# A macaron block's attention maxima: rows by transfers inside SBUF, small steps spread, sums split, two tiles normalized early

## The chip, the cores and the metric

The kernel runs on one core of a Trainium2 chip. The metric is device time in microseconds (us) from the first to the last instruction of an execution, median of the runs. Five engines work side by side, each with its own queue of instructions in a fixed order: TensorE (PE; its weight loads are PEld), VectorE (DVE), ScalarE (ACT), GpSimd (POOL) and SyncE (SP, which here only issues transfers). DMA transfers issued on SP run in the hardware queue q1, those issued on POOL in the software queue q0.

## The reference

Input x is 4 x 1024 x 512 (batches, tokens, width), float32. A half feed-forward, attention and a second half feed-forward follow one another, each on normalized rows and added to x:

```
x = x + 0.5 * ffn(layernorm(x))
x = x + attention(layernorm(x))        # 32 query heads of 16, 8 key heads, rope, softmax
x = x + 0.5 * ffn(layernorm(x))
# ffn: h = silu(x @ Wg') * (x @ Wu');  hn = h * rsqrt(mean(h*h) + eps);  hn @ Wp'
#      Wg', Wu', Wp': bf16 weights, ternary by groups of 64; hidden width 2048
# attention: w = softmax(q k^T / 4) over 1024 keys; each key head serves a group of 4 query heads
```

## The kernel before, in words

Work goes by batch b = 0 to 3. A round has three stages: a feed-forward stage (`FeedForward`) of up to three blocks of 512 tokens, the heads of attention (`Attention.run`), and a stage that projects the old attention's output and makes the next batch's queries, keys and values (`input_output`; `output` after the last). A special first feed-forward (`First`) quantizes the weights. Inside each stage the order of all engines' instructions is written out by hand (`manual_schedule`), so an engine waits where its next instruction waits.

**The heads.** The stage has 128 steps: 8 groups g of four query heads, two halves of 512 queries (qh), 8 tiles of 128 keys (kc). In step n, TensorE makes scores `s` for two pairs of heads (L1273; 512 queries by 128 keys, transposed), ScalarE takes the exponential of each pair (`e`, L1282), and TensorE weighs the values with the exponentials of the step before (eight `o` matmuls, L1289). In the first step of each half of a group, TensorE also adds the row maxima into the scores' banks: a matmul of `pick` with `even_rows` (even groups) or `odd_rows` (odd groups). Those tiles hold, in the partitions 0 to 3 and 64 to 67, minus the maximum of each query and head as a row of 1024 queries, as a high and a low part.

**The maxima.** The maxima of later groups are found ahead. `maxima` (L1126) is one item: a TensorE matmul of 128 queries by 512 keys into a bank `sm` (three of them in the heads) and a VectorE reduction to one column of `pm` (L1147). `pattern` (L1310) puts three items into each step; `more` and `READY` add a fourth if the items lag. The maxima of groups 0, 1 and most of 2 are found beside the feed-forward (`early`). When a group's 64 items are done, `subtract_maxima` (groups 0 to 5) reduces `pm` (L1169), writes high and low parts to `mst` (L1172, L1173) and leaves a function `turn` to the next step: TensorE transposes to 64 rows (`pmT`, L1181), VectorE copies them (`mrow`, L1183), POOL writes them to DRAM (`d_m`, L1185), and a later step's `maxima_in` reads them into the rows by four POOL transfers (L1221). `turn_half` (groups 6 and 7, by halves of the queries) instead puts the parts into columns of a cleared tile `spread`, transposes four 128x128 tiles (L1208) and copies the result whole into the rows (L1209), with no transfer. The two halves of group 6 are turned in steps 95 and 96, and step 96 reads the first.

**Around the heads.** SP's queue holds, in program order, the loads of the ring's places (`p_m`, `p_s`, `p_in`, `p_out`), the stores `d_o` of finished outputs, and the small transfers of `divide` (`den`, `d_r`, `rec`). Eight steps before the end, `normal_rows` makes the first token tile of the next batch (L1323); the other tiles are normalized in `input_output`, tile 1 in its first pass (L847), just ahead of its transposes (L130).

**A feed-forward's tail.** `chunks` ends with the projections of the last two hidden chunks into four banks `po` (L339 to L345). After the second bank, `factors` (L253) sums the squares of h: eight matmuls of `acc` and `sq` with a column of ones into `pq` (L259), then three small steps to the factor `half`, which `end` needs (L282).

Of the kernel before, what the change touches and what calls it, by code (L numbers as in the profile page):

```python
# [19 lines left out]
P = 128  # L20
# [17 lines left out]
def tile_macaron_block(  # L38
# [96 lines left out]
    class FeedForward:  # L135
# [116 lines left out]

        def factors(self, k):  # L253

            label = f"{self.label}_{k}"
            pq = self.ps.tile([P, 4], F32, tag="gu", name=f"pq_{label}")
            for i in range(4):
                for n, acc in enumerate(self.accs[k]):
                    nc.tensor.matmul(  # L259
                        pq[:, i : i + 1],  # L260
                        lhsT=acc[:, i * P : (i + 1) * P],
                        rhs=ones,
                        start=(n == 0),
                        stop=(n == len(self.accs[k]) - 1),
                    )
            ms = small.tile([P, 4], F32, tag="ms", name=f"ms_{label}")
            nc.vector.tensor_scalar(ms, pq, 1.0 / H, RMS_EPS, ALU.mult, ALU.add)
            inv = small.tile([P, 4], F32, tag="inv", name=f"inv_{label}")
            inverse_root(inv, ms, 4)
            half = small.tile([P, 4], F32, tag="half", name=f"half_{label}")  # L270
            nc.vector.tensor_scalar(half, inv, 0.5, None, ALU.mult)
            return half
# [33 lines left out]
        def chunks(self):  # L306
# [31 lines left out]

            for i in range(4):  # L339
                for behind in due:  # L340
                    self.project(*behind, [i])
                if i == 1:
                    half = self.factors(k)
# [4 lines left out]
    class First(FeedForward):  # L348
# [29 lines left out]
        def projection(self):  # L378

            with tc.manual_schedule():  # L380
                for c in range(2):
                    self.split(c)
                    self.parts[1, c][1]()
                for c in range(HC):
                    if c + 2 < HC:
                        self.split(c + 2)
                    self.project(1, c, self.parts[1, c][0], [0, 1])
                    self.project(1, c, self.parts[1, c][0], [2, 3])
                    if c + 2 < HC:
                        self.parts[1, c + 2][1]()  # L390
                    if 6 <= c < 10:
                        load_x(2, c - 6)
                    if c == 2:
                        at[0].first_rows()
                    if c == HC - 2:
                        half = self.factors(1)
                self.end(1, half)
# [429 lines left out]
    def input_output(new, old, put, then, wp, ps):  # L827
        turn, banks = None, 2 if put is None else 1
        puts = {4: (0,), 5: (1,), 6: (2,), 7: (3,), 8: (4,), 9: (5, 6, 7)}
        for n in range(NT + 2):  # L830
# [16 lines left out]
            if scales is not None:  # L847
                new.normalize(n + 1, wp, scales)
# [48 lines left out]
    class Attention:  # L897
# [19 lines left out]
        READY = (HKV - 1) * STEPS + NT - 3  # L917
# [3 lines left out]
        def __init__(self, b):  # L921
# [12 lines left out]
            self.early_rows = None  # L934
            self.rows, self.xTs, self.made = {}, {}, {}
            self.turning = []
# [10 lines left out]
        def first_rows(self):  # L947
# [6 lines left out]
            self.early_rows = rows  # L954

        def scales(self, i):

            if i == 0 and self.early_rows is not None:
                return None
            return normal_scales([xt[self.b, i]], f"a_{self.b}_{i}")  # L960

        def normalize(self, i, wp, scales):
            if scales is None:
                self.rows[i] = self.early_rows
# [161 lines left out]
        def maxima(self, j, ps, bufs):  # L1126
# [19 lines left out]
            def end():  # L1146
# [3 lines left out]
                done, rest = divmod(min(self.ended), self.ITEMS)  # L1150
                if min(self.ended) == before:
                    return
                if rest == self.ITEMS // 2 and g == HKV - 1:
                    self.turn_half(g, 0)
                elif rest == 0:
                    if g < HKV - 2:
                        self.subtract_maxima(g, ps, bufs)
                    else:
                        for part in range(g == HKV - 1, 2):
                            self.turn_half(g, part)  # L1160
# [4 lines left out]
        def subtract_maxima(self, g, ps, bufs):  # L1165

            b = self.b
            m = small.tile([P, NT, G], F32, tag="m", name=f"m_{b}_{g}", bufs=2)
            nc.vector.tensor_reduce(m, self.pm[g], AX.X, ALU.max, negate=True)  # L1169
            mst = small.tile([P, G, 2, NT], F32, tag="mst", name=f"mst_{b}_{g}", bufs=2)  # L1170
            by_head = m.rearrange("p i j -> p j i")
            nc.vector.tensor_copy(mst[:, :, 0, :].bitcast(F32R), by_head)  # L1172
            nc.vector.tensor_tensor(  # L1173
                mst[:, :, 1, :].bitcast(F32R), by_head, mst[:, :, 0, :], ALU.subtract
            )
            rows = G * 2 * NT
            tag = "sm" if bufs < 4 else "gu"

            def turn():
                pt = ps.tile([P, 512], F32, tag=tag, name=f"pmT_{b}_{g}", bufs=bufs)  # L1180
                nc.tensor.transpose(pt[:rows, :P], mst.rearrange("p j r i -> p (j r i)"), ident)  # L1181
                mrow = small.tile([rows, P], F32R, tag="mrow", name=f"mrow_{b}_{g}", bufs=2)
                nc.vector.tensor_copy(mrow, pt[:rows, :P])  # L1183
                self.mT[g] = dram.tile([rows, P], F32, tag="d_m", name=f"d_m_{b}_{g}", bufs=HKV)
                nc.gpsimd.dma_start(self.mT[g], mrow.bitcast(F32))  # L1185
                if g == 0:
                    self.maxima_in(g)

            self.turning.append(turn)

        def turn_half(self, g, part):

            tiles = slice(part * 4, part * 4 + 4)
            m = small.tile([P, 4, G], F32, tag="m", name=f"m_{self.b}_{g}_{part}", bufs=2)
            nc.vector.tensor_reduce(m, self.pm[g][:, tiles], AX.X, ALU.max, negate=True)
            columns = self.spread[:, tiles].rearrange("p i (e s) -> p i e s", s=PAIR)[..., :4]
            high, low = (columns[..., r::2] for r in range(2))
            m = m.rearrange("p i (a e) -> p i e a", e=2)  # L1200
            nc.vector.tensor_copy(high.bitcast(F32R), m)
            nc.vector.tensor_tensor(low.bitcast(F32R), m, high, ALU.subtract)

            def turn():
                t = self.mrows[g] = self.odd_rows if g % 2 else even_rows
                pt = self.ps.tile([P, 512], F32, tag="sm", name=f"pmT_{self.b}_{g}_{part}", bufs=3)
                for i in range(4):
                    nc.tensor.transpose(pt[:, i * P : (i + 1) * P], self.spread[:, part * 4 + i, :], ident)  # L1208
                nc.vector.tensor_copy(t[:, part * 512 : (part + 1) * 512], pt)  # L1209

            self.turning += [None, turn] if g == HKV - 1 else [turn]
# [38 lines left out]
        def run(self, keep, wp, ps):  # L1250
# [3 lines left out]
            self.spread = wp.tile([P, NT, P], F32, tag="spread", name=f"spread_{b}", bufs=1)  # L1254
# [56 lines left out]
            more = (0, 5, 10, 15)  # L1311
            late = None
            places.load(("t2", b + 1) if b + 1 < B else ("out", B))
            for n in range(HKV * self.STEPS):
# [7 lines left out]
                if n == HKV * self.STEPS - 8 and b + 1 < B:  # L1322
                    (at[b + 1].early_rows,) = normal_rows(  # L1323
                        [xt[b + 1, 0]], f"a_{b + 1}_0", keep, "rec"
                    )
                turn = self.turning.pop(0) if self.turning else None
                sides = list(pattern[n % 4]) if n > 0 else [(), ()]
                if n > 0 and n % 16 in more and self.TOTAL - sum(self.counts) > 3 * (self.READY - n):
                    sides[1] += (sides[1][0] ^ 1,)
# [7 lines left out]
                for end in ends:  # L1337
                    end()
                if late is not None:
# [5 lines left out]
                if n == 1:  # L1345
                    nc.gpsimd.memset(self.spread, 0.0)
# [111 lines left out]
```

## Time and profile before

| | us |
|---|---|
| time, median of 3 runs (lowest, highest) | 3199.89 (3199.06, 3209.4) |
| the profiled execution | 3200.95 |
| its span, from the first to the last instruction in the trace | 3199.2 |
| heads stages, from the first `o` matmuls to the last, rounds 0 to 3 | 281.7, 281.4, 281.8, 280.8 |
| TensorE busy in the window 635.5:921 (heads of round 0) | 281.58 of 285.50 |
| VectorE, ScalarE busy there | 229.95, 253.55 |
| reduction `pm<-sm` (L1147), one | 0.68 |
| `pmT<-ident,spread` (L1208), one of 64 | 0.27 |
| copy into `even_rows` or `odd_rows` (L1209), one of 16 | 0.69 |
| copy `mrow` (L1183), one of 24 | 0.28 |
| `d_m<-mrow`, issue to landing, median | 4.7 |
| rows from `d_m`, issue to landing, median (slowest) | 4.5 to 4.7 (6.3) |

The granted TensorE clock is 0.99 over the span and 1.00 in the heads. In timeline lines the columns are start, duration, engine, source line, operation, output<-inputs, shapes and count; square brackets give the engine's idle time before and what ended it.

### The profile page before, as it was taken

To read this page: it belongs to the slowest core of one execution; us is meant where nothing else is said; L and a number is where in the kernel's file an instruction comes from. 1 tells how busy PE (TensorE), PEld (TensorE's weight loads), DVE (VectorE), ACT (ScalarE), POOL (GpSimd) and SP (SyncE) were. 2 spreads that over 40 slices of the span, in tenths; PEclk is the share of its full clock that TensorE was granted. 3 is DMA by queue.
4 is the path that set the end of the run, shared out by engine and by line. 5 is a ranking of instruction groups with operands and counts; after the bars stand their busy time and mean duration, and the time that the engine had idled before them with its cause. 6 is when DMAs were issued, how large, how long until landed. Compare 5 with 4: busy or idle time off the path is not lost. (4 is left out here: it accounts for less than half of the span.)

```text
span 3199.2 us, 46128 instructions
## 1 busy us (share of the span) xinstructions
PE 3112.0 (97%) x16944; PEld 1963.6 (61%) x16944; DVE 2188.1 (68%) x3659; ACT 1758.5 (55%) x2346; POOL 951.0 (30%) x932
## 2 busy tenths in 40 slices
PE   5999899999999999999999999999999999999999
PEld 4777677733358777533377777433487776333687
DVE  7976566588855666688756665888556666887243
ACT  5752333389852333689823333898623335888343
POOL 2564333300034343201053333110243332010344
PEclk8999999999999999999999999999999999999999
DMA  3543222224324133133333222133241231332111
GB/s 111 161 125 97 88 61 78 62 76 120 111 82 129 53 93 109 45 117 102 91 107 96 87 73 70 70 110 115 86 130 60 76 96 61 97 120 65 41 60 42
DMA packets 229522, 285.64 MB, mean 89 GB/s; under 512 B 29296, under 2 KB 174704, under 8 KB 229296
## 3 DMA queue, kind: packets, MB, share of 16 engines
q1 hardware_dynamic: 220784, 271.66, 27.4%
q0 software_dynamic: 8512, 11.03, 1.6%
q8 instruction: 134, 2.20, 0.3%
q14 instruction: 92, 0.75, 0.1%
HBM read 215.74 MB, written 66.85 MB: 88 GB/s over the span
## 5 line engine op out<-in xcount | busy, mean ns | idle before, releaser
L1147 DVE TENSOR_REDUCE pm<-sm 128x1 f32<-128x512 f32 x2048 | 1281.1, 683 | 213.5 <-PE sm L1138 211.3
L1282 ACT ACTIVATE e<-s 128x1024 f32<-128x1024 f32 x1024 | 991.6, 1024 | 147.4 <-PE s L1273 138.9
L205 PE MATMUL gu<-xT,guT 128*128 128x512 f32 x1792 | 710.0, 396 | 9.9 <-DVE ql L1064 8.3
L205 PE MATMUL gu<-xL,guT 128*128 128x512 f32 x1792 | 703.2, 392 | 0.4 <-DVE xL L133 0.4
L1289 PE MATMUL o<-e,vs 128*32 128x512 f32 x4096 | 548.1, 604 | 0.0
L1138 PE MATMUL sm<-p_m,p_m 64*128 64x512 f32 x2048 | 497.1, 412 | 8.8 <-DVE h L217 6.0
L1273 PEld LDWEIGHTS s<-p_s,p_s 64*128 64x128 f32 x2048 | 193.0, 183 | 485.5 <-ACT e L1282 467.7
L1273 PE MATMUL s<-p_s,p_s 64*128 64x512 f32 x2048 | 469.0, 451 | 9.6 <-ACT e L1282 9.6
L225 POOL TENSOR_TENSOR sq<-h 128x512 f32<-128x512 f32 x210 | 218.5, 1041 | 724.1 <-DVE h L217 724.1
L217 DVE TENSOR_TENSOR h<-sg,gu 128x512 f32<-128x512 f32 x224 | 153.7, 686 | 381.2 <-PE gu L205 370.5
L215 ACT ACTIVATE sg<-gu 128x512 f32<-128x512 f32 x224 | 134.2, 599 | 480.6 <-PE gu L205 480.5
L205 PEld LDWEIGHTS gu<-xT,guT 128*128 128x128 f32 x1792 | 339.6, 190 | 84.9 <-ACT guT L94 8.7
L205 PEld LDWEIGHTS gu<-xL,guT 128*128 128x128 f32 x1792 | 339.4, 189 | 72.5 <-DVE xL L133 1.2
L245 PE MATMUL po<-w_pT,high 128*128 128x512 f32 x896 | 374.8, 418 | 0.7 <-DVE x L282 0.7
L245 PE MATMUL po<-w_pT,low 128*128 128x512 f32 x896 | 356.7, 398 | 0.2
L231 ACT CAST high<-h 128x512 fp32r<-128x512 f32 x224 | 139.1, 621 | 335.4 <-DVE h L217 323.5
L1138 PEld LDWEIGHTS sm<-p_m,p_m 64*128 64x128 f32 x2048 | 227.9, 185 | 93.9 <-DVE h L217 49.9
L229 POOL TENSOR_TENSOR acc<-acc,sq 128x512 f32<-128x512 f32 x205 | 275.8, 1346 | 16.0
L94 ACT CAST guT<-g 128x512 fp32r<-128x512 bf16 x448 | 275.0, 614 | 8.0 <-ACT guT L94 5.5
L245 PEld LDWEIGHTS po<-w_pT,high 128*128 128x128 f32 x896 | 168.7, 188 | 94.4 <-issue 56.4
L233 DVE TENSOR_TENSOR low<-h,high 128x512 fp32r<-128x512 f32 x224 | 168.6, 753 | 40.9 <-ACT high L231 40.9
L1289 PEld LDWEIGHTS o<-e,vs 128*32 128x32 f32 x4096 | 81.2, 108 | 180.9 <-issue 155.2
(166 smaller groups left out, 2934.9 us busy)
## 6 DMA issues: line engine op xcount, KB each, us to landing
g<-d_guT SPq DMA_DIRECT2D x448, 128.0 KB
p_m<-d_q SPq DMA_DIRECT2D x56, 512.0 KB
p_s<-d_q SPq DMA_DIRECT2D x56, 512.0 KB
d_o<-oT SPq DMA_DIRECT2D x64, 256.0 KB
p_m<-d_km SPq DMA_DIRECT2D x28, 512.0 KB
p_s<-d_ks SPq DMA_DIRECT2D x28, 512.0 KB
x<-in_L_attn_x_dram SPq DMA_DIRECT2D x32, 256.0 KB
w<-in_L_ffn_w_gate_up_dram SPq DMA_DIRECT2D x32, 256.0 KB
```

What stands on the lines that cost most here:

```text
L94: nc.scalar.copy(w, t)
L205: nc.tensor.matmul(pg, lhsT=self.weights[k, hc][part][:, c, :], rhs=xp[:, c, :], start=(c == 0 and low == 0), stop=(c == DC - 1 and low == 1),
L217: nc.vector.tensor_tensor(h, sg, gu[1], ALU.mult)
L225: nc.gpsimd.tensor_tensor(sq, h, h, ALU.mult)
L229: nc.gpsimd.tensor_tensor(acc, acc, sq, ALU.add)
L233: return (high, low), lambda: nc.vector.tensor_tensor(low, h, high.bitcast(F32), ALU.subtract)
L245: nc.tensor.matmul(self.pos[k][i], lhsT=h[:, i * P : (i + 1) * P], rhs=w_pT[hc], start=(hc == 0 and n == 0), stop=(hc == HC - 1 and n == 1),)
L1138: nc.tensor.matmul(s, lhsT=q[j // 2][at, i * P : (i + 1) * P], rhs=k[at, half * 512 : (half + 1) * 512], start=True, stop=True,)
L1147: nc.vector.tensor_reduce(pm[:, i, j, half : half + 1], s, AX.X, ALU.max)
L1273: nc.tensor.matmul(s[:, e, :], lhsT=lhsT[at], rhs=rhs[at, queries], start=(kc == 0 and n == 0), stop=(n == len(terms) - 1), skip_group_che ...
L1282: return w, lambda: nc.scalar.activation(w, s, AF.Exp, scale=1.0 / HD**0.5)
L1289: nc.tensor.matmul(o[j * SLOT : (j + 1) * SLOT, :], lhsT=vs[:, kc, g, :], rhs=es[j // 2][:, j % 2, :], start=(kc == 0), stop=(kc == NT - 1),)
```

## The change

Five edits:

- *Rows inside SBUF.* `turn_half` and `spread` go. Groups 3 to 7 turn through `subtract_maxima`: one transpose, one copy `mrow`, and four transfers on SP from `mrow` straight into the rows. Groups 6 and 7 do so by halves (32 rows). Groups 0 to 2 still go through DRAM.
- *Chores.* For groups 3 to 6 the three small VectorE steps are put off, one per step of the heads (`chores`), the transpose one step after the third. Groups 0 to 2 and 7 do them at once.
- *The fourth item* (`more`, `READY`) goes.
- *Two tiles early.* Where the heads normalized one tile of the next batch they now normalize two (`rows_ahead`).
- *Sums split.* In the tail of the last block of a stage, the four matmuls on `acc` come before the last projections, the four on `sq` where all eight were (`sums`). In `First.projection` both are issued in the same place as before.

```diff
+        def sums(self, k, n):
+            if n == 0:
+                self.pq = self.ps.tile([P, 4], F32, tag="gu", name=f"pq_{self.label}_{k}")
+            for i in range(4):
+                nc.tensor.matmul(
+                    self.pq[:, i : i + 1],
+                    lhsT=self.accs[k][n][:, i * P : (i + 1) * P],
+                    rhs=ones,
+                    start=(n == 0 and i == 0),
+                    stop=(n == len(self.accs[k]) - 1),
+                    skip_group_check=True,
+                )
         def factors(self, k):
...
-            pq = self.ps.tile([P, 4], F32, tag="gu", name=f"pq_{label}")
-            for i in range(4):
-                for n, acc in enumerate(self.accs[k]):
-                    nc.tensor.matmul(
-                        pq[:, i : i + 1],
-                        lhsT=acc[:, i * P : (i + 1) * P],
-                        rhs=ones,
-                        start=(n == 0),
-                        stop=(n == len(self.accs[k]) - 1),
-                    )
+            self.sums(k, len(self.accs[k]) - 1)
+            pq = self.pq
...
+            if len(self.accs[k]) > 1:
+                self.sums(k, 0)
...
+                        self.sums(1, 0)
...
-            if scales is not None:
+            if n + 1 < NT:
...
-        READY = (HKV - 1) * STEPS + NT - 3
...
-            self.early_rows = None
+            self.early_rows = {}
...
-            self.turning = []
+            self.turning, self.chores = [], []
...
-            self.early_rows = rows
+            self.early_rows = {0: rows}
+        def rows_ahead(self, keep):
+            tiles = [xt[self.b, i] for i in range(2)]
+            mv, rstd = normal_scales(tiles, f"a_{self.b}_0")
+            rows = keep.tile([P, 2, D], F32, tag="rec", name=f"xn_a_{self.b}_0", bufs=1)
+            for i, t in enumerate(tiles):
+                nc.vector.tensor_scalar(
+                    rows[:, i], t, mv[:, i, 0:1], rstd[:, i : i + 1], ALU.subtract, ALU.mult
+                )
+                self.early_rows[i] = rows[:, i]
...
-            if i == 0 and self.early_rows is not None:
+            if i in self.early_rows:
...
-                self.rows[i] = self.early_rows
+                self.rows[i] = self.early_rows[i]
...
-                done, rest = divmod(min(self.ended), self.ITEMS)
-                if min(self.ended) == before:
+                g, rest = divmod(min(self.ended) - 1, self.ITEMS)
+                if min(self.ended) == before or rest % (self.ITEMS // 2) != self.ITEMS // 2 - 1:
...
-                if rest == self.ITEMS // 2 and g == HKV - 1:
-                    self.turn_half(g, 0)
-                elif rest == 0:
-                    if g < HKV - 2:
-                        self.subtract_maxima(g, ps, bufs)
-                    else:
-                        for part in range(g == HKV - 1, 2):
-                            self.turn_half(g, part)
+                part = rest // (self.ITEMS // 2)
+                if g >= HKV - 2:
+                    self.subtract_maxima(g, ps, bufs, part)
+                elif part == 1:
+                    self.subtract_maxima(g, ps, bufs)
+                if part == 1:
...
-        def subtract_maxima(self, g, ps, bufs):
+        def subtract_maxima(self, g, ps, bufs, half=None):
...
-            m = small.tile([P, NT, G], F32, tag="m", name=f"m_{b}_{g}", bufs=2)
-            nc.vector.tensor_reduce(m, self.pm[g], AX.X, ALU.max, negate=True)
-            mst = small.tile([P, G, 2, NT], F32, tag="mst", name=f"mst_{b}_{g}", bufs=2)
+            n = NT if half is None else NT // 2
+            first = 0 if half is None else half * n
+            label = f"{b}_{g}_{first}"
+            m = small.tile([P, n, G], F32, tag="m", name=f"m_{label}", bufs=2)
+            mst = small.tile([P, G, 2, n], F32, tag="mst", name=f"mst_{label}", bufs=2)
...
-            nc.vector.tensor_copy(mst[:, :, 0, :].bitcast(F32R), by_head)
-            nc.vector.tensor_tensor(
-                mst[:, :, 1, :].bitcast(F32R), by_head, mst[:, :, 0, :], ALU.subtract
-            )
-            rows = G * 2 * NT
+            rows = G * 2 * n
...
-                pt = ps.tile([P, 512], F32, tag=tag, name=f"pmT_{b}_{g}", bufs=bufs)
+                pt = ps.tile([P, 512], F32, tag=tag, name=f"pmT_{label}", bufs=bufs)
...
-                mrow = small.tile([rows, P], F32R, tag="mrow", name=f"mrow_{b}_{g}", bufs=2)
+                mrow = small.tile([rows, P], F32R, tag="mrow", name=f"mrow_{label}", bufs=2)
...
-                self.mT[g] = dram.tile([rows, P], F32, tag="d_m", name=f"d_m_{b}_{g}", bufs=HKV)
-                nc.gpsimd.dma_start(self.mT[g], mrow.bitcast(F32))
-                if g == 0:
-                    self.maxima_in(g)
-            self.turning.append(turn)
-        def turn_half(self, g, part):
-            tiles = slice(part * 4, part * 4 + 4)
-            m = small.tile([P, 4, G], F32, tag="m", name=f"m_{self.b}_{g}_{part}", bufs=2)
-            nc.vector.tensor_reduce(m, self.pm[g][:, tiles], AX.X, ALU.max, negate=True)
-            columns = self.spread[:, tiles].rearrange("p i (e s) -> p i e s", s=PAIR)[..., :4]
-            high, low = (columns[..., r::2] for r in range(2))
-            m = m.rearrange("p i (a e) -> p i e a", e=2)
-            nc.vector.tensor_copy(high.bitcast(F32R), m)
-            nc.vector.tensor_tensor(low.bitcast(F32R), m, high, ALU.subtract)
-            def turn():
+                if g < self.FIRST:
+                    self.mT[g] = dram.tile([rows, P], F32, tag="d_m", name=f"d_m_{b}_{g}", bufs=HKV)
+                    nc.gpsimd.dma_start(self.mT[g], mrow.bitcast(F32))
+                    if g == 0:
+                        self.maxima_in(g)
+                    return
...
-                pt = self.ps.tile([P, 512], F32, tag="sm", name=f"pmT_{self.b}_{g}_{part}", bufs=3)
-                for i in range(4):
-                    nc.tensor.transpose(pt[:, i * P : (i + 1) * P], self.spread[:, part * 4 + i, :], ident)
-                nc.vector.tensor_copy(t[:, part * 512 : (part + 1) * 512], pt)
-            self.turning += [None, turn] if g == HKV - 1 else [turn]
+                for j in range(G):
+                    at = j % 2 * PAIR + j // 2 * 2
+                    nc.sync.dma_start(
+                        t[at : at + 2, first * P : (first + n) * P].bitcast(F32),
+                        mrow[j * 2 * n : (j + 1) * 2 * n, :].bitcast(F32),
+                    )
+            chores = [
+                lambda: nc.vector.tensor_reduce(
+                    m, self.pm[g][:, first : first + n], AX.X, ALU.max, negate=True
+                ),
+                lambda: nc.vector.tensor_copy(mst[:, :, 0, :].bitcast(F32R), by_head),
+                lambda: nc.vector.tensor_tensor(
+                    mst[:, :, 1, :].bitcast(F32R), by_head, mst[:, :, 0, :], ALU.subtract
+                ),
+                lambda: self.turning.append(turn),
+            ]
+            if self.FIRST <= g < HKV - 1:
+                self.chores += chores[:2] + [lambda: [f() for f in chores[2:]]]
+            else:
+                for f in chores:
+                    f()
         def maxima_in(self, g):
...
-            self.spread = wp.tile([P, NT, P], F32, tag="spread", name=f"spread_{b}", bufs=1)
...
-            more = (0, 5, 10, 15)
...
-                    (at[b + 1].early_rows,) = normal_rows(
-                        [xt[b + 1, 0]], f"a_{b + 1}_0", keep, "rec"
-                    )
+                    at[b + 1].rows_ahead(keep)
...
-                sides = list(pattern[n % 4]) if n > 0 else [(), ()]
-                if n > 0 and n % 16 in more and self.TOTAL - sum(self.counts) > 3 * (self.READY - n):
-                    sides[1] += (sides[1][0] ^ 1,)
+                sides = pattern[n % 4] if n > 0 else [(), ()]
...
+                if self.chores:
+                    self.chores.pop(0)()
...
-                if n == 1:
-                    nc.gpsimd.memset(self.spread, 0.0)
```

## The prediction

> **What bounds the kernel now.** I read the page first, then the timeline of the four heads stages, then the windows around each place that the change touches. The first block of the page:
>
> ```profile
> PE 3112.0 (97%) x16944; PEld 1963.6 (61%) x16944; DVE 2188.1 (68%) x3659; ACT 1758.5 (55%) x2346; POOL 951.0 (30%) x932
> ```
>
> TensorE is the path nearly everywhere, so only two things shorten the time: TensorE work that goes, and stretches in which TensorE is held. The page can't show the second, because a held matmul is drawn longer and stays "busy". I therefore measure steps: from one run of eight `o` matmuls to the next in the timeline. In a heads stage (128 steps, about 282 us, four times) a quiet step takes 2.12 us, and the step before a new group of heads or a new half of queries 2.58, since four matmuls with `pick` are added. The exceptions recur in every round b. The largest lies where group 6's maxima become rows (timeline of before, all engines):
>
> ```profile
> 843.32 1.06 PE L1289 MATMUL o<-e,vs 128*32 128x512 f32 x8
> ...
> 845.44 1.07 PE L1289 MATMUL o<-e,vs 128*32 128x512 f32 x8
> ...
> 845.69 0.18 DVE L1197 TENSOR_REDUCE m<-pm 128x16 f32<-128x32 f32 x1
> 845.97 0.18 DVE L1201 CAST spread<-m 128x16 fp32r<-128x16 f32 x1
> ...
> 846.79 3.07 DVE L1147 TENSOR_REDUCE pm<-sm 128x1 f32<-128x512 f32 x5
> ...
> 847.53 0.50 PE L1138 MATMUL sm<-p_m,p_m 64*128 64x512 f32 x1 [0.36 <-DVE pm L1147]
> ...
> 848.56 1.06 PE L1289 MATMUL o<-e,vs 128*32 128x512 f32 x8
> 849.56 0.66 PE L1208 MATMUL pmT<-ident,spread 128*128 128x128 f32 x4
> ...
> 851.00 0.49 PE L1273 MATMUL s<-even_rows,pick 64*128 64x512 f32 x2 [0.35 <-DVE even_rows L1209]
> ...
> 852.34 1.07 PE L1289 MATMUL o<-e,vs 128*32 128x512 f32 x8
> 853.34 0.66 PE L1208 MATMUL pmT<-ident,spread 128*128 128x128 f32 x4
> ...
> 855.20 1.06 PE L1289 MATMUL o<-e,vs 128*32 128x512 f32 x8
> ```
>
> See the starts at 845.44, 848.56, 852.34 and 855.20: steps of 3.12, 3.78 and 2.86 us where 2.12, 2.58 and 2.12 would be quiet, so 2.94 us lost. Six small VectorE steps in a row delay the reductions and TensorE runs out of `sm` banks; then two rounds of four transposes occupy it; and the new rows are read at once after their copy (0.35).
>
> Group 5 loses time in another way: its rows go through DRAM on POOL's queue and land late.
>
> ```profile
> 800.56 0.57 POOL L1185 DMA_DIRECT2D d_m<-mrow  x1 [14.46 <-DVE mrow L1183]
> ...
> 806.13 2.06 POOL L1221 DMA_DIRECT2D odd_rows<-d_m  x4 [5.00 <-DMA d_m<-mrow]
> ...
> 813.44 0.94 PE L1273 MATMUL s<-odd_rows,pick 64*128 64x512 f32 x2 [0.51 <-DMA odd_rows<-d_m]
> ```
>
> Between rounds, the second tile's normalization holds TensorE (1.10), and in a feed-forward's tail one projection waits for `low`: its start is 0.43 after the one before, where 0.23 is usual.
>
> ```profile
> 923.80 0.55 DVE L119 TENSOR_SCALAR xn_a<-x,mv_a,rstd_a 128x512 f32<-128x512 f32 x1 [19.75 <-POOL rstd_a L98]
> ...
> 924.50 0.63 PE L130 MATMUL pxn_a<-ident,xn_a 128*128 128x128 f32 x4 [1.10 <-DVE xn_a L119]
> ```
>
> **The change, part by part.** The two instruction lists side by side show that TensorE's `sm` matmuls keep their order: the rule for a fourth scan in a step, which the change drops, was never taken. It costs nothing.
>
> *Groups 3 and 4, small steps one per step.* Before, the three steps (0.22, 0.19, 0.21 us) follow one another and their step takes 2.73 to 2.74 us: 0.61 lost. After, each stands alone. In a quiet step VectorE does its three reductions in 1.89 and then idles 0.23 to 0.24 waiting for `sm`; that idle time hides one small step. Without it a step could cost its whole 0.2. I take 0. The transpose into 64 rows moves two steps later and still costs its 0.23 (706.23 to 706.46). Saved: 2 x 0.61 x 4 = 4.9. Group 5's three steps already lay in a longer step at no cost; I count nothing.
>
> *Group 5, no DRAM.* The late step takes 3.59, 3.13, 3.44 and 2.59 us in the four rounds instead of 2.58: 2.43 in all, and ScalarE, late after it, loses 0.5 more two steps on. After, the rows go from SBUF to SBUF, issued by SP two steps later than the transpose was before, still five steps (about 10 us) before they are read. No row shows such a hop on SP. Nearest: four issues at 0.32 (`d_r`) to 0.65 (`den`) each, and `den`, a 32 KB load on SP, seen by VectorE 2.2 us after its issue began (926.93 to 929.12); the worst landing of the row transfers on POOL's queue was 6.3. So 3.5 to 9 us, in time even at the slow end. Saved: 2.9.
>
> *Group 6.* Of the 2.94 us all goes: the six steps are spread, four transposes become one into 32 rows. I price that one like the 64-row transpose (0.23), twice: 0.46. Saved: 2.48 x 4 = 9.9.
> The trace has four transposes of 128x128 in 0.66 us, starting some 0.15 apart. The Trainium skill (TensorE: Matmul & The Clock Gate, Part 4: PE-mode transpose) measured about 275 ns for one in a kernel's context; a single record here agrees (273), but counted end to end by that rule the sixteen of a round would cost 4.4 us instead of 2.3, and the four rounds would save some 8 us more than the overlapped rows say. The step lengths above already hold what is true here.
>
> *Group 7, first half.* Its transposes and their copy (0.69) make a step of 2.86: 0.74 lost, 0.23 stays. Its small steps fall where they did, in the longer step that hid them. Saved: 0.5 x 4 = 2.0.
>
> *Group 7, second half.* Maxima are over by then and ScalarE sets the pace. The four transposes open 0.54 us of ScalarE idle where 0.2 is usual, so I take 0.25 (0 to 0.54): 1.0. Here a new wait enters. The rows must be on chip by the next half of queries. Counted from the `o` matmuls at 897.07, the transpose ends at about +1.3, the copy at +1.7, four issues at +3.7, and the landing comes at +5.5 to +6; they are read at about +7.4. It holds with 1.4 us to spare; with a landing of 6.3 it is late by 2.7. I take 0.
> These four transfers now stand on SP behind the `p_out` loads (1.5 MB, issued 890.94 to 895.35). The windows show the DMA engines at 0.99, 0.93 and 0.61 in the 2 us slices from 892, and 0.02 from 898: they are through before my issue at about 899. The Trainium skill (DMA: Bandwidth & Descriptors, Queues, rings and completion order) says that SP has one ring on each DMA engine, consumed in order, which speaks against moving the rows to SP; by that rule rows issued 3 us earlier would wait, and here the sum stays as it is.
>
> *Two tiles normalized in the heads.* Three rounds (not the first, not the last stage). The extra statistics lie in steps 120 onwards, where VectorE idles over 15 us. TensorE then turns tile 1 at once; what is late next is ScalarE's copy of tile 0, which ends at 924.08, so the projection starts at about 924.25 instead of 924.96. Saved: 0.7 x 3 = 2.1 (0 to 1.1 each).
>
> *Sums split.* Same matmuls; four of them move ahead of the last projections and fill the wait for `low`: 0.20 of wait and 0.11 of a slower restart. The block of sums breaks TensorE's run twice now; leaving it costs about 0.1 (0.32 to the second projection after it, not 0.23). Saved 0.2 in each of five tails (-0.1 to 0.3): 1.0. The first projection's sums keep their place.
>
> Cleared `spread` (POOL, 0.97) and POOL's row transfers go, hidden anyway.
>
> **The sum**: 4.9 + 2.9 + 9.9 + 2.0 + 1.0 + 2.1 + 1.0 = 23.8. The profiled execution took 3200.95 us (span 3199.2), 1.1 above the median 3199.89: 3200.95 - 23.8 = **3177**. About 0.3% (9.6 us) is what a measurement can tell from no change.
>
> **Rivals.**
> - *Late at the last deadline.* The rows of group 7's second half land as slowly as POOL's did. For it: the margin of 1.4 us is the smallest. Against: SP's small load took 2.2. Up to 2.7 x 4 = 11: **3188**.
> - *Small steps not hidden.* Fifteen per round are spread over steps with 0.24 us of cover; if each costs its 0.2, 60 x 0.2 = 12: **3189**. Against: group 5's three cost nothing in one longer step, and a bank's reuse leaves 0.28 us more.
> - *ScalarE takes over.* If ScalarE bounded the steps as soon as TensorE's holds go, the gain shrinks to what lies outside steps and group 5: some 6, **3195**, no measurable change. Against: per eight steps ScalarE has 8 x 1.94 + 0.59 = 16.1 us, TensorE 8 x 2.12 + 0.46 = 17.4.
> - *SP's queue turns the gain over (slower).* Group 6's second half stands behind `den`, which itself waits for `d_o` to land (6.3 to 7.2 us). The rows should land at +13 after the `o` matmuls at 852.34, and are read at +16.9. With the slowest landing they are 1.1 late. If they also drain behind a stage's weight loads (6.4 us from 890.9 to 897.3) there and at the last deadline, a round loses 1.1 + 2.7 + 2 x 6.4 = 16.6, less 6 saved: (16.6 - 6) x 4 = 42, **3243**. From 6 us of lateness a round it is slower. Against: issue order puts the `p_in` loads after, the `p_out` loads well before.
>
> **How the numbers follow.** Forecast 0.75, late deadline 0.10, small steps 0.07, ScalarE 0.05, SP's queue 0.03. The first three are faster by over 0.3%: faster 0.92, same 0.05, slower 0.03. The range takes in the tails and tiles at their best (another 0.5 + 1.2 + 1.2, and some for neighbouring steps) and, above, the two slower cases that are still faster: 3171 to 3189.
>
> **What would show it.** Right: steps of at most 2.2 us where the small steps are, one short `pmT` per half, no `odd_rows` wait at the start of group 5, the second `pxn_a` straight after the first, no gap before the tail's `low`. Wrong: TensorE waiting for `odd_rows` or `even_rows` landings in the last groups (late hop), steps of 2.3 in threes (cover gone), or ScalarE without idle time between its activations.

## The result and the profile after

| | before | after |
|---|---|---|
| time, median of 6 runs each (lowest, highest), us | 3200.54 (3199.06, 3209.4) | 3228.38 (3223.49, 3235.61) |
| after / before | | 1.0085, 95% interval 1.0068 to 1.0101 |
| the profiled execution (its span) | 3200.95 (3199.2) | 3223.49 (3221.7) |
| heads stages, rounds 0 to 3 | 281.7, 281.4, 281.8, 280.8 | 290.8, 287.8, 289.7, 285.9 |
| all that lies outside them | 2073.4 | 2067.5 |

The change made the kernel slower, by 0.85%; 3177 was forecast, and the range ended at 3189. The profiled execution of after is the fastest of its six; the other five left no trace, so the waits told of below may be longer there.

First block of the page of after, to set beside that of before:

```profile
PE 3103.9 (96%) x16896; PEld 1961.1 (61%) x16896; DVE 2178.1 (68%) x3656; ACT 1758.8 (55%) x2346; POOL 914.9 (28%) x865
```

TensorE is busy for 8 us less while the span is 22 us longer: it stands. The list of all waits of after names the place (engine, line, what was waited for: sum, times, longest):

```profile
PEld s L1288 <- DMA odd_rows<-mrow: 31.4, 4, 10.1
...
PE s L1288 <- DMA odd_rows<-mrow: 30.3, 4, 9.8
...
PE s L1288 <- DMA even_rows<-mrow: 7.1, 4, 2.1
```

Each occurs four times, once a round (PE and PEld wait side by side, so their rows are not added). Where before lost 2.94 us at group 6, the timeline of after (TensorE) reads:

```profile
846.55 1.06 PE L1304 MATMUL o<-e,vs 128*32 128x512 f32 x8
...
848.67 1.07 PE L1304 MATMUL o<-e,vs 128*32 128x512 f32 x8
...
857.18 1.07 PE L1304 MATMUL o<-e,vs 128*32 128x512 f32 x8
...
859.76 1.06 PE L1304 MATMUL o<-e,vs 128*32 128x512 f32 x8
...
861.88 1.06 PE L1304 MATMUL o<-e,vs 128*32 128x512 f32 x8
862.88 0.28 PE L1196 MATMUL pmT<-ident,mst 128*32 128x128 f32 x1
...
864.21 1.07 PE L1304 MATMUL o<-e,vs 128*32 128x512 f32 x8
...
874.85 1.07 PE L1304 MATMUL o<-e,vs 128*32 128x512 f32 x8
878.42 0.88 PE L1288 MATMUL s<-even_rows,pick 64*128 64x512 f32 x2 [2.08 <-DMA even_rows<-mrow]
...
879.95 1.06 PE L1304 MATMUL o<-e,vs 128*32 128x512 f32 x8
```

The small steps and the four transposes cost nothing more (2.12 and 2.58 us where 3.12, 3.78 and 2.86 stood; the one transpose, at 862.88, makes its step 2.33), but the rows of group 6's second half now come late: 5.10 us between the last two `o` lines, 2.58 would be quiet. At the start of group 5 it is far worse. From here on, step n is the time from the n-th run of eight `o` matmuls of a heads stage to the next. Step 79, where `odd_rows` is read (timeline of after, all engines):

```profile
795.49 0.52 SPq L758 DMA_DIRECT2D p_m<-d_km  x1
...
802.66 0.27 DVE L1198 CAST mrow<-pmT 64x128 fp32r<-64x128 f32 x1
...
802.96 6.92 SPq L1208 DMA_DIRECT2D odd_rows<-mrow  x4
...
809.95 1.06 PE L1304 MATMUL o<-e,vs 128*32 128x512 f32 x8
...
809.98 1.16 SPq L1107 DMA_DIRECT2D rec<-d_r  x1
...
821.23 0.94 PE L1288 MATMUL s<-odd_rows,pick 64*128 64x512 f32 x2 [9.78 <-DMA odd_rows<-mrow]
...
822.27 1.02 ACT L1297 ACTIVATE e<-s 128x1024 f32<-128x1024 f32 x1 [10.93 <-PE s L1288]
...
823.63 1.93 PE L1304 MATMUL o<-e,vs 128*32 128x512 f32 x8
```

From the start of the issue to the read: 18.3 us, where 3.5 to 9 had been forecast. What the DMA engines did in that time is in the windows of after (us, busy time of the engines, TensorE's clock, share of the 16 DMA engines, GB/s):

```profile
796.00:800.00 4.00, 4.00 (x30) 1.39 (x28) 3.62 (x9) 3.84 (x6) 0.00 (x0) 1.00 0.95 302
800.00:804.00 4.00, 4.00 (x31) 1.73 (x31) 3.58 (x8) 3.38 (x5) 0.00 (x0) 1.00 0.14 53
804.00:808.00 4.00, 4.00 (x34) 1.52 (x30) 3.52 (x6) 3.63 (x5) 0.00 (x0) 1.00 0.13 48
...
812.00:816.00 4.00, 0.00 (x0) 0.00 (x0) 0.00 (x0) 0.00 (x0) 0.00 (x0) 0.94 0.44 132
816.00:820.00 4.00, 0.00 (x0) 0.00 (x0) 0.00 (x0) 0.00 (x0) 0.00 (x0) 0.50 0.13 47
```

Taken together they are not busy: a share of 0.13 is two engines of sixteen (0.125), and these two move 48 GB/s without a pause. The page lists `p_m<-d_km` and `p_s<-d_ks` as single transfers of 512 KB; at 48 GB/s one takes 10.9 us, and the timeline has one at 785.43 and the next at 795.49. In the trace's packets 4 KB ones run without a break from 800, and the rows' packets, of 512 bytes, come only at 817.3 to 818.0 and 819.9 to 820.7. Up to then the two engines have moved some 770 KB since 800 (16 us at 48 GB/s, an estimate): the load of 795.49 and a part of the one of 785.43. `rec`, issued on the same queue after the rows, went ahead of them: from 812 to 816 the share is 0.44, and no other transfer that SP had in flight could add 4 KB packets there.

**Theory.** The key loads, issued as one transfer to both halves of the partitions (outermost dimension 2), run on two DMA engines. A row transfer goes to two partitions, so it runs on the same two engines, and there SP's queue serves it after the loads ahead of it. The Trainium skill (DMA: Bandwidth & Descriptors, section "Why a DMA increments its semaphore by 16 and not by 1", How many engines) states such a rule: the number of engines is the largest up to 16 that divides the outermost dimension (the first of size above 1) of both sides, and on SP's queue they are the lowest-numbered ones. The share of 0.13 agrees with it; the packets carry no engine number, so which two they are is not shown.

**Rivals.** The hop inside SBUF is slow by itself; SP issues too late (`den` ahead of it, 6.92 us for four issues); the DMA system as a whole is too loaded; the key loads hold the kernel whatever is done with the rows.

### The profile page after: what moved, and what is told of

Same layout as the page of the kernel before. It is cut to its first block, busy times and chain, and to the rows that moved or that the text cites. A ratio compares the mean times of both kernels' runs of the same rounds, so it can differ in the third digit from the quotient of the medians.

```text
span 3221.7 us, 46141 instructions
## 1 busy us (share of the span) xinstructions
PE 3103.9 (96%) x16896; PEld 1961.1 (61%) x16896; DVE 2178.1 (68%) x3656; ACT 1758.8 (55%) x2346; POOL 914.9 (28%) x865
```

## Experiments

All times are medians, with the ratio to before and its 95% interval where there were enough runs.

### The rows on POOL's queue

The four row transfers of a turn:

```diff
-                    nc.sync.dma_start(
+                    nc.gpsimd.dma_start(
```

> The changed kernel with its SBUF-to-SBUF row transfers issued by POOL instead of SP, nothing else. Theory R (ring): the rows' transfers run on two of the sixteen DMA engines and stand there, in SP's ring, behind the key loads, which use the same two; on POOL's queue they have rings of their own, land within 2 to 5 us, the steps at the start of group 5 and of group 6's second half fall to 2.58 us, and the time is 3223.5 - 49.6 = 3174 (3172 to 3180). Rival H (hop): small pieces from SBUF to SBUF on two engines are slow wherever issued; the long steps stay and the time is 3215 to 3235. Rival S (SP): the rows are late because SP, which works in order and waits for earlier transfers, issues them late; then this also gives about 3174.

Measured: 3180.33, ratio 0.9938 (0.9921 to 0.9954). Step 103 is quiet, step 79 takes 2.58 to 3.49, and the rows land 1.7 to 5.5 us (medians) after their issue, with the same key loads in flight. So neither the hop as such nor the DMA system as a whole makes the 18 us: it goes with SP's queue. Which engines POOL's transfers used is not known. But a new step appears, 85, with 3.0 to 3.8 us (timeline of this kernel):

```profile
822.39 2.38 POOL L1110 TENSOR_TENSOR aT<-aT,rec 128x1024 f32<-128x1024 f32 x1 [17.23 <-DMA rec<-d_r]
...
822.67 2.13 DVE L1217 CAST mst<-m 128x16 fp32r<-128x16 f32 x1
...
825.45 1.09 PE L1157 MATMUL sm<-p_m,p_m 64*128 64x512 f32 x2 [0.60 <-DVE pm L1166]
```

The put-off cast usually takes 0.18; begun during POOL's multiplication it ends with it. This happened in all four rounds (2.13, 2.25, 1.40, 2.13), since `rec`, which POOL's multiplication waits for, lands just then. Why the two exclude each other was not tried.

### Each key load as two transfers

The two stand where the one transfer was issued:

```diff
-        sources.append(keys.unsqueeze(0).to_broadcast([2, PAIR, T]))
+        for e in range(2):
+            nc.sync.dma_start(tiles[2].bitcast(F32)[e * PAIR : (e + 1) * PAIR, at], keys[:, at])
```

> The changed kernel, rows on SP as they are, but each load of the keys (512 KB, one transfer whose outer dimension is 2) is issued as two transfers of 64 partitions. Theory R: the key loads then use all engines, the two engines' backlog of about 17 us goes, the rows land in time: 3174 (3172 to 3182). Rival S: SP has more to issue, not less, so the rows are as late as now or later: 3223 to 3240. Rival H: unchanged, 3220 to 3235.

Measured: 3165.14, ratio 0.9891 (0.9876 to 0.9906). Steps 79 and 103 are quiet (2.58) in every round, though the rows stand where they stood, on SP. The four heads stages take 276.1 each, 21.4 us less than before in all; the terms for the heads summed to 20.7. No turn's four issues took over 3.2 us (6.92 at step 79's turn in after). Outside the heads it is another 8 us faster than after, which was not expected. Most of that is in TensorE's waits there (for `ql` 7.8 in after, 2.7 here; of `sm` for `h` 7.4 and 5.5) and in its clock, which was halved for 20 us outside the heads of after and for 14 us here (between 100 and 3100 us).

### The rows on ScalarE's queue

```diff
-                    nc.sync.dma_start(
+                    nc.scalar.dma_start(
```

> The changed kernel with the row transfers issued by ScalarE. Theory R: another ring on the same two engines, so the rows no longer wait behind the whole key load and land in a few us; 28 issues a round on ScalarE at 0.3 to 0.6 us each are mostly hidden, since ScalarE has about 1.3 us to spare in eight steps, but a turn's four issues come in one step: 3174 to 3195. Rival H: 3215 to 3240.

Measured: 3326.84, ratio 1.0396 (1.0375 to 1.0417): a miss. The heads now lose time at every turn, 2.4 to 8.3 us (timeline of this kernel):

```profile
711.66 6.95 ACTq L1208 DMA_DIRECT2D odd_rows<-mrow  x4
...
718.00 0.64 SPq L1096 DMA_DIRECT2D den<-d_o  x1
...
718.71 1.02 ACT L1297 ACTIVATE e<-s 128x1024 f32<-128x1024 f32 x1 [7.40 <-DMA odd_rows<-mrow]
```

The four issues take 6.95 us, and the exponentials queue behind them. On SP, in after, four took as long (6.92), and no engine that computes stood behind them. They end about when SP's `den`, which awaits the landing of `d_o`, starts; what exactly an issue waits for was not tried. The time says nothing against the theory: the first packet of group 5's rows came 4.5 to 5.4 us after the first issue and the last 11.3 to 12.8, where SP in after had 12.0 to 14.3 and 14.0 to 17.7.

### Before, with each key load as two transfers

The same edit, on the kernel before.

> The kernel before with the key loads split as above and nothing else. Theory R: before, nothing on TensorE's path waits in SP's ring on the two engines, so 3197 to 3201; at most the 2.9 us that group 5's rows lose on POOL's queue go as well, if their packets shared those engines. Rival: key loads on two engines hold the kernel by themselves, and it becomes clearly faster, under 3190.

Measured: 3185.11, ratio 0.9954 (0.9939 to 0.9969): a miss. In the heads only step 79 and 81 change, as expected (280.7 each). Outside them 14 us go. In the first feed-forward TensorE waited 8.32 us for `ql`, now 2.69: ScalarE's `high`, on which that hangs, waited 11.9 us for the key store `d_ks<-ql` to land, now 6.3, and these stores stand in SP's queue behind a key load (issued at 312.55 before). TensorE's clock was halved for 34 us outside the heads of before and for 10 us here (between 100 and 3100 us), which is worth 12 us at most (half of the difference, an estimate). So the last rival is right in part: the key loads cost the kernel before 16 us already, and the change added rows to what stands behind them.

### One key load of a round at a time

The edit of the two transfers on after, but only where `(kind, g) == ("m", 7)`, and then only where `(kind, g) == ("s", 7)`.

> The changed kernel with the two-transfer load for one key tile of each round only: group 7's `p_m<-d_km`, the one issued just ahead of group 5's rows. Theory (the rows stand behind the key load that the queue of SP put on the same two DMA engines): step 79, where `odd_rows` is awaited, falls from 10.05 to 13.68 us to 2.58 to 2.6, while step 103, whose rows stand behind group 7's `p_s<-d_ks`, stays at 4.3 to 5.8 us; time about 3223 - 39.6 = 3184, or up to 9 less if this load also held work outside the heads. Rival (the queue of SP is loaded as a whole, any relief helps all): both steps shrink by a part. Rival (the row transfers are slow by themselves on two engines): both stay.

> The inverse: the two-transfer load for group 7's `p_s<-d_ks` only. Theory: step 103 falls to 2.58 us, step 79 stays at 10 to 13.7 and step 80 at 2.6 to 3.9; time about 3223 - 10 = 3213. Rival (the queue as a whole): both shrink by a part.

Measured: 3192.33 and 3218.05, one run each, so that the steps and not these times carry the reading. Waits of the first kernel, then of the second, as far as they concern the turned rows:

```profile
PE s L1302 <- DMA even_rows<-mrow: 9.6, 4, 2.9
```

```profile
PE s L1302 <- DMA odd_rows<-mrow: 31.7, 4, 11.0
```

With `p_m` split, step 79 is quiet (once 3.01) and step 103 stays at 4.2 to 6.7; with `p_s` split it is the reverse: 103 quiet, 79 at 10.6 to 14.9. So each late read goes away when the nearest load ahead of it is split and the other is left as it is. The rival of a queue that is loaded as a whole falls.

The two are late in different ways. At step 79 SP issues the rows as soon as `mrow` is there (802.96, after 802.66 + 0.27), and their packets wait. At step 103 SP issues them late: `mrow` is there at 863.6 both in after and with `p_s` split (timeline of SP in after):

```profile
861.50 0.32 SPq L1314 DMA_DIRECT2D d_o<-oT  x1
...
869.95 0.64 SPq L1096 DMA_DIRECT2D den<-d_o  x1
...
870.68 2.67 SPq L1208 DMA_DIRECT2D even_rows<-mrow  x4
```

With `p_s` split, `d_o` is issued at 861.54 as in after (to 0.04 us), but `den` already at 863.56 and the four rows at 864.30 (2.69 us long). `den`, ahead of the rows, waits for `d_o` to land. In after 112 of the 128 packets of `d_o` went from 862.3 to 863.2 and the last 16 only at 868.8 to 869.4, after the 4 KB packets of the key load; 16 of 128 is two engines' share of sixteen. From issue to last packet the rows take 7.0 us in after and 7.3 with `p_s` split, so here the issue was late and not the hop. The rival that SP issues too late is right for step 103, with the key load as its cause, and wrong for step 79.

### The small steps at once

On the kernel with all key loads in two transfers:

```diff
-            if self.FIRST <= g < HKV - 1:
-                self.chores += chores[:2] + [lambda: [f() for f in chores[2:]]]
-            else:
-                for f in chores:
-                    f()
+            for f in chores:
+                f()
```

> The kernel with all key loads in two transfers, and the three small VectorE steps of every group done at once again. By the prediction's terms: steps 30 and 51 back from 2.13 to 2.73 us, 0.61 x 8 = 4.9; group 5's three steps lie in a longer step at no cost; for group 6, whose halves now turn apart, three steps in a row should cost 0.6 per half where the step is a quiet one, at most 4.9 more. So 3170 to 3175 against 3165. Rival (the small steps cost their 0.2 wherever they stand, spread or not): no difference, 3165.

Measured: 3175.67, ratio 0.9921 (0.9905 to 0.9938). Steps 30 and 51 return to 2.73, and the two halves of group 6 cost 0.53 each (steps 83 and 94, 2.12 to 2.65); all heads together 9.5 us. Spread, the small steps are free, and at once they cost what the steps of before showed.

### The tile, the sums, and where the buffers lie

On the kernel with all key loads in two transfers; first both edits undone, then the tile alone:

```diff
-            tiles = [xt[self.b, i] for i in range(2)]
+            tiles = [xt[self.b, i] for i in range(1)]
...
-            if len(self.accs[k]) > 1:
-                self.sums(k, 0)
...
                 if i == 1:
+                    if len(self.accs[k]) > 1:
+                        self.sums(k, 0)
                     half = self.factors(k)
```

> The kernel with all key loads in two transfers, with one tile normalized early instead of two, and the eight matmuls of the sums together again. By the prediction's terms: 2.1 for the tile and 1.0 for the sums, so 3168, with a gap of 1.1 us before the second tile's `pxn_a` in three rounds where 0.73 stands now, and 0.43 between the projection that waits for `low` and the one before. Rival (these places don't set the end): 3165 and the same gaps.

Measured: 3179.94, ratio 0.9934 (0.992 to 0.9949): a miss by 12 us. Two things came out. The tail, from the start of the last `gu` matmul to the end of the last projection, takes 8.08 instead of 7.75, a little more than priced, but in one round 9.58 (timeline of this kernel, TensorE; then its windows, the clock third from the right):

```profile
1305.92 0.95 PE L258 MATMUL pq<-ones,acc 128*128 128x1 f32 x8
1306.73 1.03 PE L258 MATMUL pq<-ones,sq 128*128 128x1 f32 x8
1307.62 0.63 PE L245 MATMUL po<-w_pT,high 128*128 128x512 f32 x1
1308.05 0.63 PE L245 MATMUL po<-w_pT,low 128*128 128x512 f32 x1
```

```profile
1305.00:1307.50 2.50, 2.50 (x20) 2.32 (x19) 0.00 (x0) 0.00 (x0) 0.00 (x0) 1.00 0.00 0
1307.50:1311.00 3.50, 3.50 (x11) 2.45 (x10) 2.02 (x4) 0.00 (x0) 2.66 (x4) 0.54 0.00 0
```

After eight short matmuls twice in a row the granted clock is 0.54 over 3.5 us, and the projections start 0.43 apart instead of 0.23. And the first `pq` comes 5.1 to 7.0 us after the last `o` matmuls, where the kernel before has 2.7: undoing the tile costs far more than the tile had saved. The next run shrinks its buffer, `[P, 2, D]` to `[P, 1, D]`, and leaves the sums split:

> The kernel with all key loads in two transfers, with one tile normalized early and its buffer as small as it was before the change (one tile, not two), the sums still split. In the run that undid both edits around the heads, ScalarE's copy `axT_a` waited 2.7 us more in each round, for the landing of `d_o<-oT`, since the copy's buffer lay where `oT` had been. If that wait came from where the buffers happened to lie, the first `pq` comes 2.72 to 2.75 us after the last `o` matmuls as before, 0.33 a round later than with two tiles: 3165 + 1 = 3166. If it came from normalizing the second tile late at all, the first `pq` stays at 5 us or more: 3173.

Measured: 3179.31, ratio 0.9927 (0.9909 to 0.9945), `pq` still at 5.1 to 7.4: not the size of that buffer. Timeline of this kernel:

```profile
912.55 0.33 SPq L1323 DMA_DIRECT2D d_o<-oT  x1
...
915.24 0.59 ACT L131 COPY axT_a<-pxn_a 128x512 f32<-128x512 f32 x1 [2.71 <-DMA d_o<-oT]
...
915.88 0.66 PE L130 MATMUL pxn_a<-ident,xn_a 128*128 128x128 f32 x4 [3.40 <-ACT axT_a L131]
```

The copy waits for the landing of a store whose data it does not use; what the two can share is memory. The last run of this row puts back `spread`, unread:

```diff
+            self.spread = wp.tile([P, NT, P], F32, tag="spread", name=f"spread_{b}", bufs=1)
...
+                if n == 1:
+                    nc.gpsimd.memset(self.spread, 0.0)
```

> The kernel with all key loads in two transfers and one tile normalized early, and with the tile `spread` of the kernel before allocated and cleared again, though nothing reads it. A smaller buffer for the early tile did not take away ScalarE's wait of 2.7 us for the landing of `d_o<-oT`. Theory (the next stage's buffers lie on the memory of the heads stage; without `spread` the copy `axT_a` falls on `oT`): the first `pq` comes 2.72 to 2.75 us after the last `o` matmuls, as before the change, and the time is about 3179 - (2.7 + 3.0 + 5.0) = 3168 or less. Rival (the wait has nothing to do with where the buffers lie): `pq` at 5 to 7 us, 3179.

Measured: 3165.39, ratio 0.9893 (0.9877 to 0.991), `pq` at 2.71 to 2.74:

```profile
909.64 0.33 SPq L1324 DMA_DIRECT2D d_o<-oT  x1
909.66 0.58 ACT L131 COPY axT_a<-pxn_a 128x512 f32<-128x512 f32 x1
```

So an unread tile takes the wait away, which says that without `spread` the copy's buffer lies on memory of `oT` (addresses were not looked at). Why two tiles normalized early take it away too was not tried; perhaps the buffer of a later tile falls there, which has time.

### Group 0's rows inside SBUF as well

On the kernel with all key loads in two transfers, the turn of group 0 takes the path of the later groups, on POOL's queue:

```diff
-                if g < self.FIRST:
+                if 0 < g < self.FIRST:
...
-                    nc.sync.dma_start(
+                    (nc.sync if g else nc.gpsimd).dma_start(
```

> The kernel with all key loads in two transfers, and group 0's rows, which are made in the feed-forward, no longer through DRAM but straight from `mrow` by four transfers on POOL's queue. With DRAM, POOL waits for the landing of `d_m` (1.5 us) and issues four more transfers (2.1 us) ahead of `rstd` of the next block's tile; VectorE waits for that with `xn`, `h` is late behind it, and TensorE stands 1.1 us, once 2.05 with a half clock for 3.4 us after it. If these go: 1.1 x 2 + 1.3 + 2.05 + 1.7 = 7 at most, 3158 to 3161. Rival (VectorE would have been late anyway, by its reductions): 3164 to 3166, and the gap before `sm` of 1.1 us stays.

Measured: 3156.98, ratio 0.9857 (0.9841 to 0.9873), the fastest kernel here: 1.4% faster than before. The waits of 1.1 to 2.0 us before `sm` are gone in every round, and with them the half clock that followed the longest one.

## Why the prediction was wrong, point by point

The terms against the trace; heads by their steps, the last column in the kernel with all key loads in two transfers, us:

| term | forecast | after | two transfers |
|---|---|---|---|
| groups 3 and 4 (steps 30 to 34, 51 to 55) | -4.9 | -5.0 | -5.0 |
| group 5 (steps 79 to 82) | -2.9 | **+36.7** | -2.9 |
| group 6, first half (83 to 97) | -9.9 | -10.1 | -10.1 |
| group 6, second half read (103, 104) | 0 | **+10.0** | 0.0 |
| group 7, first half (105 to 107) | -2.0 | -2.2 | -2.1 |
| group 7, second half (108 to 127) | -1.0 | -1.6 | -1.6 |
| two tiles early | -2.1 | -1.0 | -1.0 |
| sums split, five tails | -1.0 | -3.1 | -3.1 |
| other steps, and the rest outside the heads | 0 | -1.2 | -9.9 |
| sum | -23.8 | +22.5 | -35.7 |

- **The step that failed** is in group 5: "So 3.5 to 9 us, in time even at the slow end." The hop's price was taken from one load of SP at another place (`den`, 2.2) and from POOL's queue (6.3). What the runs showed in its place: 14.6 to 18.3 us from issue to read, since the rows, on SP, wait behind 512 KB key loads on two engines; with the nearest of these loads in two transfers the read is on time. The room was smaller too: the kernel with all key loads in two transfers reads the rows 8.3 us after their issue, not about 10, so that the slow end of 9 would not have been in time. The queue was looked at only before the last deadline, where a share of 0.02 did mean idle engines. Ahead of group 5's rows the kernel before shows the key load (0.16 from 804 to 808, 0.13 from 812 to 816): two engines at their limit look like that. The late hop was among the prediction's signs of being wrong.
- Besides the wait itself, the 10 us in which TensorE stands let its clock fall to 0.50, and step 80 loses 4.0 us in the four rounds.
- **Group 6's second half** was named in the rival "SP's queue turns the gain over", by the wait of `den` for `d_o`. That wait is there (`mrow` at 863.60, issue at 870.68; 6.9 to 7.1 us in the four rounds), and the last packet comes 6.2 to 7.0 us after the issue. Why `d_o` lands late the rival did not have: taking only the `p_s` load off the two engines makes the read timely. It was right in direction and in this wait, wrong in what the queue drains (it named weight loads, it was key loads), in the other place (it named the last deadline, it was group 5) and in size: 49.6 us of lateness in four rounds, 12.4 a round, above its turning point of 6 but below its 16.6.
- The last deadline, the margin of 1.4 us that was feared most, held in all rounds (in the last one the read came 5.8 us after the issue and the last packet 3.3).
- Small steps, transposes, one turn of 0.23 per half: right to a few tenths, and confirmed from the other side by doing them at once.
- **Two tiles**: 0.33 a round, not 0.7. The second tile's transposes wait 0.73 for ScalarE's copy of the first (1.10 before), and the projection comes only 0.33 earlier. That this edit also kept the copies off the store of `oT`, worth 2.3 to 4.6 us a round without `spread`, was not foreseen.
- **Sums**: 0.32 a tail, not 0.2, and 1.5 more in the one tail of before whose clock fell to 0.52. That part is luck: it struck one tail of five.

What stays open: what an issue of the row transfers waits for (6.9 us for four, at most 3.2 once all key loads are in two transfers), and how the 10 us of the row "other steps, and the rest outside the heads" divide between TensorE's waits and its clock.

## What to carry to other kernels

A transfer moved to another queue inherits all that stands ahead of it there, the waits of the issuing engine as well, and what counts is on which engines the loads ahead run, not their bytes alone: a load broadcast over an outermost dimension of 2 ran on two engines, and one issue more made it harmless. A low DMA share ahead of a late transfer is a reason to look for such a load, not to rule out the DMA. An edit that frees a buffer can move the buffers behind it: look for new waits on stores in places that the edit does not touch.

## What the runs showed of the hardware

- A load of 512 KB whose source is broadcast over an outermost dimension of 2 moved 48 GB/s at a DMA share of 0.13; as two transfers of 64 partitions the same load left the rows behind it in time.
- SP's queue is not served in order as a whole: in after `rec`, issued at 809.98, moved from 812 on, and the rows, issued from 802.96 on, only from 817.3; and 112 of the 128 packets of the store `d_o` went some 6 us ahead of the other 16.
- TensorE's clock: where it stood from 811 to 821 in after it was halved from 815.5 to 825.8, until almost 5 us after work had begun again. Sixteen one-column matmuls in a row were followed by 3.4 us at half clock in 3 of 15 tails (three kernels); with the block split in two, in none of 50 tails (ten kernels). The Trainium skill (TensorE: Matmul & The Clock Gate, Part 1) tells of a free-running window of about 3.4 us in which the activity is judged; the 3.4 us and that it strikes only some tails agree with it.
- VectorE's cast from SBUF to SBUF of 0.18 us took up to 2.25 while POOL multiplied 128x1024 elements; reductions from PSUM beside it did not slow down (0.68 to 0.69 each).
- Four DMA issues in ScalarE's queue held its exponentials for 7.4 us, at other turns for up to 8.2.
